# A two-layer graph kernel: layer 0 of all graphs first, then layer 1 in quads by two levels of Strassen

## The chip, the core and the metric

The kernel runs on one NeuronCore of a Trainium2 chip. The metric is the device time of one execution in microseconds (us). Everything is float32.

## The reference, cut to what matters

There are 128 graphs of 128 nodes with 512 features. `x` is [128, 128, 512], `adj` [128, 128, 128]. Both layers add their result to `x`.

```
# layer 0
h = relu(layernorm(x))
Xw = h @ Wv + bv;  sj = Xw @ aw[:512];  si = Xw @ aw[512:]
t = adj * exp(leaky_relu(sj[None, :] + si[:, None] + ab, 0.2));  t = t / (row sums of t + 1e-12)
H = (h @ Wk[0] + bk[0]) + (t @ h @ Wk[1] + bk[1]) + (t @ t @ h @ Wk[2] + bk[2])
x = x + relu(H)
# layer 1
h = relu(layernorm(x))
q, k = split(h @ Wqk);  v = h @ Wv1
w = rowsum(q * (adj @ (k * mask))) * mask / sqrt(512)
x = x + softmax(w over the nodes)[:, None] * v
```

The kernel never forms q and k. It folds the two halves of Wqk into one 512x512 matrix M, so that w is the row sum of (h @ M) * (adj @ h), scaled. Layer 1 is thus h @ [M, Wv1], a 512-deep product with 1024 columns, and one aggregation of h per graph.

## The kernel before, in words

Graphs are taken in pairs (G = 2, 64 pairs, p = 0 to 63). A dense product of a pair has two row blocks (the graphs), two halves of the 512-deep contraction and two halves of the columns. `strassen` (line 325) computes it with seven block products for eight, by the Winograd form. The left sums are made by `left_sums` (lines 313 to 323), four VectorE additions of 128x512 elements as two halves; the right sums are made once by `combine` (line 166). The seven products are accumulated in four PSUM banks a, b, c, e, and three copies by ScalarE (lines 343, 345, 347, 351) hand partial sums from one bank to the next. Each block product is two matrix instructions, one per 128-deep chunk (line 336). There are eight PSUM banks by name: set1 is a1, b1, c1, e1, and set2 is a2, b2, c2, e2.

For pair p, the work is this.

- `norm0(p)` (line 355): layer norm and relu (`norm_relu`, lines 255 to 281), written to DRAM and read back in 32x32 blocks (`by_blocks`, lines 288 to 297), so that `begin(p)` can transpose it on VectorE (line 302) and make the left sums.
- `y2(p)`: h @ Wk[2] with the attention columns, a Strassen product with 257-wide halves in set2. Then the column of sj is spread over the partitions: a small VectorE transpose into `pzt` (line 380), a DMA to DRAM `pzd` (line 382) and a DMA that reads it back on all partitions as `pz` (line 384), both issued by GpSimd.
- `attention(p)`: adds `pz` and si (line 398), leaky relu, exp, times adj, row sums, division; gives t. It also makes A^T of the pair by a VectorE transpose (line 412).
- `y10(p)`: h @ [Wk[1], Wk[0]], a Strassen product with 512-wide halves in set1, seeded with the biases (`seed_a`, `seed_e`); `t_transposed(p)` transposes t on TensorE within it.
- `inner(p)` and `outer(p)`: two times four products of 256 columns with t^T, then relu and the sum with x (line 73) into x1.
- `norm2`: layer norm of x1 into h2, and again the way through DRAM for its transpose.
- `layer1(p)`: h2 @ [M, Wv1], a Strassen product with 512-wide halves in set2, and two aggregations adj @ h2 of 512 columns, with A^T as the left side (line 474). `score` (line 560) takes the row sums, `spread_scores` (line 563) spreads them by way of DRAM, `weights` (line 575) makes the softmax, and `result` (line 593) multiplies, adds x1 and writes out.

The loop runs over p. Its body issues y10(p), inner(p), y2(p+1), the end of the layer 1 of pair p-2, outer(p), and then layer1(p-1) and attention(p+1). Layer 1 of the pair before thus stands between one pair's y2 and the next pair's y10. Tile pools hand out the buffers. The order of the instructions on each engine is set when the program is built: a scheduler with costs of its own orders them within the data dependencies, and `issue_after` pins some of them by hand (`behind`, line 70). At run time each engine takes its queue in that order.

## Time and profile before

| | |
|---|---|
| median of three runs | 2319.53 us (2315.21 to 2322.03) |
| profiled execution, its own time | 2314.45 us |
| span of the profiled execution, first to last instruction | 2312.7 us |
| TensorE (PE) busy | 2303.2 us |
| VectorE (DVE) busy | 1362.6 us |
| ScalarE (ACT) busy | 1026.8 us |
| GpSimd (POOL) busy | 341.9 us |
| data moved by DMA | 241.55 MB, 104 GB/s |

A group of the profile names line, engine, operation and tiles (output <- inputs), then the count, the busy time in us and the mean duration of one in ns, and last the time that the engine stood idle just before such instructions, with what released it. A matrix instruction in float32 leaves two records. PE durations overlap, since the matrix products are pipelined: the distance between starts is their pace.

### The profile page before, as it was taken

To read this page: it belongs to the slowest core of one execution; us is meant where nothing else is said; L and a number is where in the kernel's file an instruction comes from. 1 tells how busy PE (TensorE), PEld (TensorE's weight loads), DVE (VectorE), ACT (ScalarE), POOL (GpSimd) and SP (SyncE) were. 2 spreads that over 40 slices of the span, in tenths; PEclk is the share of its full clock that TensorE was granted. 3 is DMA by queue.
4 is the path that set the end of the run, shared out by engine and by line. 5 is a ranking of instruction groups with operands and counts; after the bars stand their busy time and mean duration, and the time that the engine had idled before them with its cause. 6 is when DMAs were issued, how large, how long until landed. Compare 5 with 4: busy or idle time off the path is not lost.

```text
span 2312.7 us, 23740 instructions
## 1 busy us (share of the span) xinstructions
PE 2303.2 (100%) x6889; PEld 1291.1 (56%) x6889; DVE 1362.6 (59%) x4134; ACT 1026.8 (44%) x2514; POOL 341.9 (15%) x595
## 2 busy tenths in 40 slices
PE   9999999999999999999999999999999999999999
PEld 5555555555555555555555555555555555555554
DVE  5665656655656566566565665565665656656654
ACT  4444444444444444444444444444444444444443
POOL 3011111111111111111111111111111111111100
PEclk9999999999999999999999999999999999999999
DMA  7343333333333333333333333333343333333321
GB/s 192 106 124 103 93 117 93 109 104 101 111 106 90 121 91 108 112 98 108 105 96 116 93 103 112 98 108 105 98 115 99 97 114 96 110 103 100 110 64 51
DMA packets 247060, 241.55 MB, mean 104 GB/s; under 512 B 25822, under 2 KB 171486, under 8 KB 246930
## 3 DMA queue, kind: packets, MB, share of 16 engines
q1 hardware_dynamic: 225632, 212.26, 30.4%
q0 software_dynamic: 21152, 27.65, 5.5%
q8 instruction: 54, 0.88, 0.2%
q14 instruction: 76, 0.62, 0.1%
q10 hardware_dynamic: 146, 0.14, 0.0%
HBM read 140.20 MB, written 99.74 MB: 104 GB/s over the span
## 4 chain that ended last, share of the span: by engine, by line
PE 98%; DMA 1%; DVE 1%; issue 0%; ACT 0%; POOL 0%; DVEq 0%; SPq 0%
PE b L336 24%; PE c L336 24%; PE a L336 24%; PE e L336 12%; PE a L474 2%; PE e L474 2%; PE a L452 1%; PE b L452 1%; PE b L462 1%; PE e L462 1%; PE c L452 1%; PE c L462 1%; PE e L452 1%; PE a L462 1%; PE a L423 1%; DMA t<-in_L_gnn_Wv_dram 1%
## 5 line engine op out<-in xcount | busy, mean ns | idle before, releaser
L336 PE MATMUL a<-r,x 128*128 128x257 f32 (+1 forms) x1024 | 372.7, 486 | 0.1
L93 POOL DMA_DIRECT2D agb<-in_adj_dram x256 | 152.2, 599 | 825.4 <-DVE t L409 780.3
L374 DVE TENSOR_TENSOR y<-e,s 128x257 f32<-128x257 f32 x64 | 27.3, 427 | 401.7 <-ACT s L351 401.7
L336 PEld LDWEIGHTS a<-r,x 128*128 128x128 f32 x1024 | 189.4, 190 | 105.8 <-issue 92.1
L336 PE MATMUL a<-rl,x 128*128 128x512 f32 x504 | 236.8, 592 | 0.0
L351 ACT COPY s<-c 128x512 f32<-128x512 f32 (+1 forms) x191 | 97.4, 510 | 207.9 <-PE c L336 207.8
L336 PE MATMUL b<-t,sx 128*128 128x257 f32 (+1 forms) x512 | 186.4, 486 | 2.7 <-ACT b L343 2.7
L336 PE MATMUL b<-r,sx 128*128 128x257 f32 (+1 forms) x512 | 186.5, 486 | 0.0
L336 PE MATMUL c<-t,sx 128*128 128x257 f32 (+1 forms) x512 | 186.4, 486 | 0.0
L336 PE MATMUL c<-t,x 128*128 128x257 f32 (+1 forms) x512 | 186.2, 486 | 0.0
L336 PE MATMUL e<-t,sx 128*128 128x257 f32 (+1 forms) x512 | 186.1, 486 | 0.0
L382 POOL DMA_DIRECT2D pzd<-pzt x62 | 36.9, 595 | 941.3 <-DVE pzt L380 910.6
L347 ACT COPY c<-b 128x512 f32<-128x512 f32 (+1 forms) x191 | 95.2, 499 | 179.1 <-PE b L336 177.6
L345 ACT COPY s<-e 128x512 f32<-128x512 f32 (+1 forms) x191 | 98.4, 515 | 156.2 <-PE e L336 156.2
L302 DVE STREAM_TRANSPOSE x<-hv 128x512 f32<-128x512 f32 x252 | 163.5, 686 | 1.9 <-DMA hv<-hd 1.7
L336 PEld LDWEIGHTS a<-rl,x 128*128 128x128 f32 x504 | 95.8, 190 | 93.2 <-issue 89.9
L268 DVE TENSOR_TENSOR r<-r 128x2 f32<-128x2 f32 x128 | 20.0, 156 | 203.2 <-ACT r L267 203.1
L343 ACT COPY b<-a 128x512 f32<-128x512 f32 (+1 forms) x191 | 95.6, 500 | 94.8 <-PE a L336 87.2
L336 PEld LDWEIGHTS b<-t,sx 128*128 128x128 f32 x512 | 97.1, 190 | 71.4 <-issue 46.4
L336 PEld LDWEIGHTS c<-t,x 128*128 128x128 f32 x512 | 97.0, 190 | 68.5 <-issue 61.2
L336 PEld LDWEIGHTS c<-t,sx 128*128 128x128 f32 x512 | 96.9, 190 | 68.6 <-issue 60.3
L336 PEld LDWEIGHTS e<-t,sx 128*128 128x128 f32 x512 | 96.9, 189 | 68.4 <-issue 60.7
(231 smaller groups left out, 3926.6 us busy)
## 6 DMA issues: line engine op xcount, KB each, us to landing
hd<-h SPq DMA_DIRECT2D x126, 512.0 KB, 2.8
hv<-hd SPq DMA_DIRECT2D x504, 128.0 KB, 2.9
xg<-in_x_dram SPq DMA_DIRECT2D x63, 512.0 KB, 3.8
out_dram<-x SPq DMA_DIRECT2D x63, 512.0 KB, 4.2
ag<-in_adj_dram SPq DMA_DIRECT2D x64, 128.0 KB, 2.6
agb<-in_adj_dram POOLq DMA_DIRECT2D x256, 32.0 KB, 2.1
pw<-pwd POOLq DMA_DIRECT2D x63, 128.0 KB, 3.3
pz<-pzd POOLq DMA_DIRECT2D x62, 128.0 KB, 3.5
```

The costliest lines, as they stand in the source:

```text
L93: nc.gpsimd.dma_start(agb[p][c * S32:(c + 1) * S32].rearrange("p g q i -> p (g q) i"), v[c])
L302: nc.vector.transpose(dst[:, j].rearrange("p f (n b) -> p f n b", n=Q), hv[:, j].rearrange("p n (f a) -> p f n a", f=Q))
L336: done["product"] = nc.tensor.matmul(bank, left[i][:, k * P:(k + 1) * P], right[i][:, k], start=(start and k == 0), stop=(k == HC - 1), sk ...
L343: nc.scalar.copy(b, a)
L345: nc.scalar.copy(s[:, 0], e)
L347: done["u2"] = nc.scalar.copy(c, b).ins
L351: nc.scalar.copy(s[:, 1], c)
L374: (1, 1): lambda e, t: nc.vector.tensor_add(y[:, 1, 1], e, t),
L382: nc.gpsimd.dma_start(d.rearrange("g q b -> q g b"), t[::S32])
L452: nc.tensor.matmul(bank[:, :HD], TT[p][:, j, :], y[:, j, nh, 1 - nh:W2 - nh], start=False, stop=True, skip_group_check=True)
L462: nc.tensor.matmul(bank[:, HD:], tt[:, j, :], z[:, j, nh], start=False, stop=True, skip_group_check=True)
L474: nc.tensor.matmul(to, AT[p][:, j, :], h2, start=True, stop=True)
```

## The change

Two loops take the place of one. The first runs layer 0 of all 64 pairs and ends each pair by writing four things to DRAM: h2 (`H2D`), its transpose (`XD`), the scaled A^T (`ATD`) and x1 (`X1D`). During pairs 2 to 9 the right side of layer 1 is worked out to the second level: seven matrices of 128x7x256 elements, kept in DRAM (`RWD`); four of them are loaded during pair 10, three after the loop.

The second loop takes four graphs (a quad, two pairs) at a time, 32 in all. The outer level of Strassen is over the two pairs and the halves of the contraction and gives seven factors; the inner level is over the two graphs of a pair and again halves. That is 49 products of a 128x128 left with a 128x256 right, one matrix instruction each. The outer factors 1, 5 are done in set1 and 2, 6 in set2 in step with each other, then the four aggregations, then 3, 7 in set1 and 4 in set2. The left sums are made in two levels, the outer ones on GpSimd (`load_left`), the inner on VectorE (`inner_sums`). Adding the outer factors up is left to VectorE and GpSimd (`adding_ends`). The scores of a quad are spread together, and the sum with x1 is made by an accumulating DMA from GpSimd's queue.

In the first loop, y2(p+2) follows outer(p), attention(p+1) follows y10(p), and the temporaries of y2 and y10 (`s2` and `s0` before) share one buffer `s`.

The core of the diff:

```diff
     def y2(p):
-        s = front.tile([P, 2, WP], FP, name="s2", bufs=1)[:, :, :W2]
+        s = front.tile([P, 2, WP * 2], FP, name="s", bufs=1)[:, :, :W2]
...
     def y10(p, steps):
-        s = front.tile([P, 2, D], FP, name="s0", bufs=1)
+        s = front.tile([P, 2, WP * 2], FP, name="s", bufs=1)[:, :, :D]
...
+    def for_layer1(p):
+        hT = front.tile([P, G, DC, N], FP, name="x2", bufs=1)
+        transposed(HV2.pop(p), hT)
+        for j in range(G):
+            nc.sync.dma_start(XD[p][:, :, j].rearrange("k p n -> p k n"),
+                              hT[:, j].rearrange("p (k f) n -> p k (f n)", k=2))
...
+    def norm2(p):
+        HV2[p] = by_blocks(norm_relu(X1[p]), H2D[p])
...
+    for p in range(NP):
+        def lefts():
+            if p == 0:
+                behind("t", begin, 1)
+                behind("left", norm0, 2)
+                return
             if p + 2 < NP:
+                begin(p + 2)
+            for_layer1(p - 1)
             if p + 3 < NP:
+                norm0(p + 3)
+
+        y10(p, {1: lefts, 6: lambda: behind("product", t_transposed, p)})
+        if 0 < p and p + 1 < NP:
+            attention(p + 1)
+        z = inner(p)
...
+        outer(p, z)
...
+        if p + 2 < NP:
+            y2(p + 2)
+        if p + 1 < NP:
+            seed_a()
+            seed_e()
+        norm2(p)
...
+    def load_left(q, pool):
+        f = F[q] = pool.tile([P, 8, G, HC, N], FP, name="f")
+        fv = f.rearrange("p o j k n -> p o (j k n)")
+        for o, p, kh in ((1, 2 * q, 0), (2, 2 * q, 1), (L21, 2 * q + 1, 0), (4, 2 * q + 1, 1)):
+            at = L21 if o == L21 else SLOT[o]
+            nc.sync.dma_start(fv[:, at], XD[p][kh].rearrange("p g n -> p (g n)"))
+        at = {o: fv[:, i] for o, i in SLOT.items()}
+        nc.gpsimd.tensor_add(at[5], fv[:, L21], at[4])
+        nc.gpsimd.tensor_sub(at[6], at[5], at[1])
+        nc.gpsimd.tensor_sub(at[3], at[2], at[6])
+        nc.gpsimd.tensor_sub(at[7], at[1], fv[:, L21])
+
+    def inner_sums(q, pool, first, n):
+        v = F[q][:, first:first + n]
+        s = pool.tile([P, 4, n, N], FP, name=f"in{first}")
+        b = {(j, k): v[:, :, j, k] for j in range(G) for k in range(2)}
+        nc.vector.tensor_add(s[:, 0], b[1, 0], b[1, 1])
+        nc.vector.tensor_sub(s[:, 1], s[:, 0], b[0, 0])
+        nc.vector.tensor_sub(s[:, 2], b[0, 0], b[1, 0])
+        nc.vector.tensor_sub(s[:, 3], b[0, 1], s[:, 1])
...
+    def adding_ends(to, other):
+        def one(i, j):
+            return lambda a: nc.vector.tensor_add(to(i, j), a, other(i, j))
+        def two(i, j):
+            def end(e, t):
+                nc.vector.tensor_add(t, e, t)
+                nc.gpsimd.tensor_add(to(i, j), t, other(i, j))
+            return end
+        return {(0, 0): one(0, 0), (1, 1): two(1, 1), (0, 1): two(0, 1), (1, 0): one(1, 0)}
...
+    def spread_scores(col):
+        t = small.tile([P, S32], FP, name="pwt", bufs=1)
+        nc.vector.transpose(t, col)
+        d = dram.tile([S32, Q, S32], FP, name="pwd")
+        nc.gpsimd.dma_start(d.rearrange("g q b -> q g b"), t)
+        dst = back.tile([P, 2 * G, N], FP, name="pw", bufs=1)
+        nc.gpsimd.dma_start(dst.rearrange("p g n -> p (g n)"), bcast(d, 0, 2 * G * N))
+        return dst
...
+    def result(q):
+        c, w = C.pop(q), W.pop(q)
+        factors = weights(w, spread_scores(w))
+        for pair in range(2):
+            v = c[:, pair].rearrange("p j h d -> p j (h d)")
+            for j in range(G):
+                at = pair * G + j
+                nc.scalar.activation(v[:, j], v[:, j], AF.Copy, scale=factors[:, at:at + 1])
+            p = 2 * q + pair
+            nc.gpsimd.dma_start(v, X1D[p].rearrange("g n d -> n g d"), accum_op=OP.add)
+            nc.sync.dma_start(out[p * G:(p + 1) * G].rearrange("b n d -> n b d"), v)
...
+    for q in range(NQ):
...
+        inner_sums(q, back, 4, 3)
+        together(one_round(q, set1, (1, 5), s1, plain_ends(lambda i, j: c[:, 0:2, i, j])),
+                 one_round(q, set2, (2, 6), s2, adding_ends(
+                     lambda i, j: c[:, 2:4, i, j],
+                     lambda i, j: c[:, 0:1, i, j].to_broadcast([P, 2, HD]))))
+        nc.vector.tensor_add(c[:, 0].rearrange("p j h d -> p (j h d)"), c[:, 3].rearrange("p j h d -> p (j h d)"),
+                             c[:, 1].rearrange("p j h d -> p (j h d)"))
+        for i, bank in enumerate((a1, a2, e1, e2)):
+            pair, j = divmod(i, 2)
+            ordered(lambda: nc.tensor.matmul(bank, AT[q][:, pair, j], H2[q][:, pair, j], start=True, stop=True))
+            nc.scalar.copy(agg[:, pair, j], bank)
+        scores(q, 0, c[:, 2])
+        if q > 0:
+            result(q - 1)
+        if q + 1 < NQ:
+            load_left(q + 1, fpools[(q + 1) % 2])
+            load_rest(q + 1)
+        together(one_round(q, set1, (3, 7), s1, adding_ends(lambda i, j: c[:, 0::3, i, j],
+                                                            lambda i, j: c[:, 0::3, i, j])),
+                 one_round(q, set2, (4,), s2, adding_ends(lambda i, j: c[:, 2:3, i, j],
+                                                          lambda i, j: c[:, 3:4, i, j])))
+        nc.gpsimd.tensor_add(c[:, 1].rearrange("p j h d -> p (j h d)"), c[:, 3].rearrange("p j h d -> p (j h d)"),
+                             c[:, 1].rearrange("p j h d -> p (j h d)"))
+        if q + 1 < NQ:
+            inner_sums(q + 1, early, 0, 4)
+        scores(q, 1, c[:, 2])
+    result(NQ - 1)
```

`one_round` issues seven products for its factors with the copies and ends of `strassen`; `together` puts the steps of two rounds side by side.

## The prediction

> **What bounds the kernel now.** I read the page's busy line and its chain first.
>
> ```profile
> PE 2303.2 (100%) x6889; PEld 1291.1 (56%) x6889; DVE 1362.6 (59%) x4134; ACT 1026.8 (44%) x2514; POOL 341.9 (15%) x595
> ...
> PE 98%; DMA 1%; DVE 1%; issue 0%; ACT 0%; POOL 0%; DVEq 0%; SPq 0%
> ```
>
> TensorE is never idle and is 98% of the chain. So the time is the number of matrix instructions times their pace, and the pace is in the timeline of PE alone, in the distances between starts.
>
> ```profile
> 1000.14 1.03 PE L336 MATMUL e<-t,sx 128*128 128x257 f32 x4
> 1001.01 1.03 PE L336 MATMUL b<-t,sx 128*128 128x257 f32 x4
> ...
> 1005.78 0.59 PE L462 MATMUL e<-zz,tt 128*128 128x256 f32 x2
> 1006.21 0.59 PE L462 MATMUL b<-zz,tt 128*128 128x256 f32 x2
> ...
> 1007.07 1.88 PE L336 MATMUL a<-rl,x 128*128 128x512 f32 x4
> 1008.79 1.88 PE L336 MATMUL e<-tl,sx 128*128 128x512 f32 x4
> ...
> 1042.56 1.88 PE L336 MATMUL a<-rl,x 128*128 128x512 f32 x4
> ```
>
> Four records are two instructions: 512 columns cost 1.717/2 = 0.858 us, 257 columns 0.433, 256 columns 0.432. A pair repeats every 35.49 us (1042.56 - 1007.07). Check: 28 x 0.858 + 14 x 0.433 + 8 x 0.432 + 2 x 0.858 (aggregations) + 0.22 (two transposes) = 35.5.
>
> Next, how full the others are while PE is full, from one 36 us window (PE, PEld, DVE, ACT, POOL, clock, DMA share, GB/s), and how long the spreading of the attention column takes, from the timeline of all engines.
>
> ```profile
> 1036.00:1072.00 36.00, 36.00 (x111) 20.34 (x110) 21.00 (x64) 16.07 (x40) 5.27 (x9) 1.00 0.37 108
> ```
>
> ```profile
> 1005.96 0.24 DVE L380 STREAM_TRANSPOSE pzt<-y 128x64 f32<-128x64 f32 x1 [0.20 <-ACT y L376]
> ...
> 1006.49 0.59 POOL L382 DMA_DIRECT2D pzd<-pzt  x1 [15.26 <-DVE pzt L380]
> ...
> 1008.42 0.57 POOL L384 DMA_DIRECT2D pz<-pzd  x1 [1.33 <-DMA pzd<-pzt]
> ...
> 1018.30 0.35 DVE L398 TENSOR_SCALAR s<-pz,y,cz 128x128 f32<-128x128 f32 x1
> ```
>
> ```profile
> pw<-pwd POOLq DMA_DIRECT2D x63, 128.0 KB, 3.3
> pz<-pzd POOLq DMA_DIRECT2D x62, 128.0 KB, 3.5
> ```
>
> pzt ends at 1006.20; pz is issued at 1008.42 and lands 3.5 us later, at 1011.9: a way of 5.7 us. VectorE takes pz up at 1018.30, so 6.4 us of slack lie behind it. Those 12 us are filled with twenty other VectorE instructions, many of them layer 1's.
>
> **What the Trainium skill says.** *GPSIMD Engine Reference*, 3.1: a two-input float32 `tensor_tensor` of 2048 elements takes 4497 ns on GpSimd, about 2.2 ns an element. The trace of before has no such instruction; I estimate 1.2 us for 512 elements and 2.3 for 1024. *SBUF — State Buffer*, Who interferes with whom: a VectorE instruction with two SBUF inputs contends with a GpSimd instruction that reads SBUF, and the second to start blocks until the first ends. No run here shows it; I leave it for the range. *TensorE: Matmul & The Clock Gate*, What's actually happening: an idle window of about 3.4 us can halve TensorE's clock. The trace only shows 1.00 with no gaps.
>
> **The change, part by part.**
>
> *Products.* A quad has 49 x 0.432 + 4 x 0.858 = 24.60 us, where two pairs had 56 x 0.432 in products and the same aggregations: 2.9 us less a quad. A pair of layer 0 keeps 14 x 0.858 + 6.06 + 3.46 + 0.22 = 21.75. Together 64 x 21.75 + 32 x 24.60 = 2179 for 64 x 35.49 = 2271: 92 us gained, if PE still sets the pace. The matrix rate for narrower products is not in doubt, since 256-wide ones already run at 0.432 back to back.
>
> *Layer 0 alone.* VectorE is 21.0 x 35.49/36 = 20.7 us busy per pair. Taking out layer 1's rows (left sums, two adds, scores, result, softmax; 7.1 by their means, 6.5 with the overlap of neighbours) and adding nothing, since h2's transpose stays, about 14.5 remain: 67% of 21.75. That fits by share, but not by order. I looked at how the built program orders VectorE's queue. Before, in 61 of 62 pairs 19 or 20 places lie from `pzt` to the first use of `pz`. Now it is the very next instruction in 22 pairs, 2 to 5 places on in 16, 6 to 10 in 20 (often the next pair's transposes and left sums, 2.6 us) and over 10 in 4. The queue is in order, so the 5.7 us are waited out: 22 x 5.7 + 16 x 4.5 + 20 x 3.1 = 259, or 4.2 us a pair. Behind this wait stand the next pair's transposes and left sums and the addition to e1 that `inner` needs, so TensorE gets it in full.
>
> Further waits of a middle pair, laid out by hand in queue order: `pzt` needs ScalarE's last copy of y2, which in half of the pairs stands behind the two h2 activations (2 x 0.76), 1.0 on average; VectorE waits for ln and exp of the norm, now behind a y2 copy, 1.7; the shared `s` puts y10's copies of e and c behind y2's end, and small dependent instructions 0.2 apart instead of 0.16, together 2.5. Sum: 14.5 + 4.2 + 1.0 + 1.7 + 2.5 = 23.9, taken as 24.0, a pair against 21.75 of PE. Lower bound 21.75, upper 27 (every pair with a full wait).
>
> DMA: about 4.2 MB a pair (x, adj twice, h and h2 out and back, h2^T, A^T, x1, pz) in 24 us is 173 GB/s, by 0.37 x 173/108 a share of 0.6. SP issues some 16 DMAs at 0.4 us (timeline), 7 of 24 us; h comes back within about 8 us and is used more than 10 later. Hidden, unless latencies grow; then pz's does too.
>
> *Second-level right sides.* 4 x 1.22 + 28 x 0.42 = 17 us of VectorE over eight pairs, which has no room left: 17.
>
> *Layer 1 alone.* Again there is a ring through VectorE's queue. `pwt`(q) is followed by two ends and then the maximum over pw(q). Between stand GpSimd's DMA to DRAM (0.2 + 0.6), then, ahead of the DMA that reads it back, the four outer left sums of a later quad (4 x 1.2 + 0.2), then that DMA (0.1 + 3.6 for twice the bytes of before): 9.6 us, of which none is needed sooner. From the maximum to the next `pwt` I lay out, in queue order: maximum 0.7, three ends 2.0, softmax with four exps 0.4, left sums and ends up to the second score 6.0; then VectorE waits for round 3, whose copies stand in ScalarE's queue behind four agg copies and four scalings of c (0.57 and 0.76 each, to 9.3), so that a1 ends at 12.2; seven ends to 17.2; the score waits for GpSimd's last additions, 19.1; two scores, one end, four sums and `pwt` to 23.2. Ring: 23.2 + 9.6 = 32.8, say 33 against 24.60. Without the additions between, and with ScalarE prompt, 25; with GpSimd and VectorE blocking each other, 36. 31 x 33 + 27 for the first = 1050. No row shows an accumulating DMA: between the 4.2 us of a plain write of 512 KB and twice that. It is issued some 10 us into the ring and its buffer c is wanted again 13 us or more later, write included, so I take nothing, and up to 2 us a quad for the upper end.
>
> *Ends.* Start as before, 33 us to the first y2. Between the loops 15: the last transposes and the three factors, 2.75 MB at the 231 GB/s of the first window (12). After the last product 18 more than before: score, two DMAs, softmax, four scalings, accumulating DMA, write.
>
> *Sum.* 33 + 64 x 24.0 + 17 + 15 + 1050 + 18 = 2669, as a span. Around the span lie 1.8 us (2314.45 - 2312.7), and the profiled run is 5 us under the median, so about 2675. I take 2670.
>
> **Rivals.** 0.3% is about what a measurement of this kernel can tell from no change.
>
> - *PE stays the bound* (faster). The mechanism is slack in buffers: x has three, h and y2 two, so VectorE may be carried ahead over the pz way, and in layer 1 the ends may lie under the next rounds. Then 2313 - 92 + 17 for the ends and 10 for the right sides = 2248. It decides if both rings come in under 21.75 and 24.60. For it: VectorE's share is 67% in layer 0 and about 80% in layer 1 (19.6 of 24.6 us, by the means of like rows). Against it: waits in an in-order queue are not share, and both rings close through VectorE. 4%.
> - *Only layer 0 loses*: the layer 1 ring under 24.6, 33 + 1536 + 17 + 15 + 787 + 18 = 2406. 11%.
> - *Only layer 1 loses*: 33 + 1392 + 17 + 15 + 1050 + 18 = 2525. 15%.
> - *Both, and worse*: pz late under 0.6 DMA share, the engines' lock, TensorE's clock halved after gaps over 3.4 us: 27 and 36 give 33 + 1728 + 17 + 15 + 1143 + 18 = 2954. 9%.
> - *Both as worked out*: 2670, from 2560 to 2800. 61%.
>
> That the change doesn't do what it says is excluded: the built queue has 49 products a quad.
>
> **How the numbers follow.** The likeliest is 2670. Leaving out the first case, most of the second and the upper half of the fourth gives 2450 to 2880. Faster 0.04, within 0.3% 0.01, slower 0.95.
>
> **What would show it.** Layer 0: the use of pz with a wait for DMA in VectorE's list, 3 to 6 us for many pairs; PE idle before `inner` with VectorE as releaser; pair distance near 24. Layer 1: the maximum waiting for pw; quad distance near 33; PE's product distance 0.432 throughout. Wrong: PE near 100% in either loop, GpSimd additions far from 1.2 us, or a wait for hv or f, which would be DMA.

## The result, and the profile after

The changed kernel takes 2886.99 us (median of four runs, 2883.29 to 2889.57), where the kernel before took 2317.66 us beside it (median of four). The ratio is 1.245, with a 95% interval of 1.243 to 1.248. That is slower, as forecast, by 7 us more than the upper end of the range (2880) and by 217 us more than the value (2670).

From the page of the changed kernel, the busy line, TensorE's clock in 40 slices, and the chain:

```profile
PE 2438.2 (84%) x8223; PEld 1585.9 (55%) x8223; DVE 1588.1 (55%) x4223; ACT 1236.3 (43%) x2929; POOL 791.3 (27%) x886
...
PEclk9999999999999999999999998989898989888887
...
issue 12%; POOL 11%; PE 10%; DMA 7%; DVE 7%; ACT 5%; POOLq 0%; SPq 0%; ACTq 0%; DVEq 0%
```

TensorE was 98% of the chain and is now 10% of it; the other shares of the line go round between all engines and the DMA. No engine is full. So the time lies in engines that wait for one another. Where such waits close into a ring (each waits for the next and the last for the first), the length of the ring is the pace, and the question is where it closes. The first product of layer 1 starts at 1730.09 us, so the two loops can be read apart. From the view by stretches (PE, PEld, DVE, ACT, POOL, then clock, DMA share, GB/s):

```profile
36.00:1730.00 1694.00, 1497.79 (x4740) 893.27 (x4739) 924.08 (x3009) 738.85 (x1782) 220.95 (x376) 0.96 0.57 163
1730.00:2888.00 1158.00, 909.39 (x3394) 674.20 (x3392) 647.13 (x1163) 485.42 (x1124) 555.88 (x476) 0.88 0.50 135
```

A pair of layer 0 takes (1730 - 33)/64 = 26.5 us (26.3 without the 17 us forecast for the right sides), forecast 24.0. Layer 1 takes 1158 us, forecast 15 + 1050 + 18 = 1083. VectorE is busy 55 and 56%.

*Layer 0.* The list of waits between 100 and 1750 us (engine, line and tile, releaser: total, times, longest):

```profile
DVE z L418 <- DMA pz<-pzd: 417.4, 60, 10.5
...
PE c L349 <- ACT s L364: 103.3, 47, 5.7
```

VectorE waits 7 us for `pz` in nearly every pair. How TensorE gets it is seen in the timeline of one pair, around 1300 us:

```profile
1295.92 0.25 DVE L401 STREAM_TRANSPOSE pzt<-y 128x64 f32<-128x64 f32 x1 [1.51 <-ACT y L397]
...
1301.72 0.60 POOL L405 DMA_DIRECT2D pz<-pzd  x1 [4.69 <-DMA pzd<-pzt]
1305.53 0.60 DVE L418 TENSOR_SCALAR z<-pz,y,cz 128x128 f32<-128x128 f32 x2 [9.36 <-DMA pz<-pzd]
1307.57 3.53 PE L349 MATMUL c<-t,x 128*128 128x512 f32 x4 [2.40 <-ACT s L364]
```

`pzt` is ready at 1296.2, and VectorE does nothing until 1305.5. The exp of the attention stands ahead of a copy in ScalarE's queue and waits for `z`, so the copy comes late and TensorE stands idle 2.40 us; then it runs at half pace (3.53 us for four records that took 1.88 in the profile shown before). The way from the end of `pzt` to the landing of `pz` took 5.7 us in the pair that the prediction read, and 6.0 in the mean over 62 pairs of the kernel before. Here it is 8.7 in the mean. The list of DMAs shows it too (count, KB, median us from issue to landing), first from the changed kernel's page, then from the kernel before between 700 and 1500 us:

```profile
pz<-pzd POOLq DMA_DIRECT2D x62, 128.0 KB, 4.3
pzd<-pzt POOLq DMA_DIRECT2D x62, 1.0 KB, 3.3
...
pzd<-pzt POOLq DMA_DIRECT2D x22, 1.0 KB, 1.7
```

`pz` lands in 4.3 us, where it was 3.5; the write of 1 KB ahead of it takes 3.3, where it was 1.7.

*Layer 1.* The list of waits between 1800 and 2880 us:

```profile
DVE peak L731 <- DMA pw<-pwd: 262.6, 31, 9.3
...
PE e L797 <- DVE s L715: 146.6, 30, 5.6
```

and one turn of the ring in the timeline:

```profile
2203.05 0.20 DVE L746 STREAM_TRANSPOSE pwt<-wcol 128x32 f32<-128x32 f32 x1
...
2203.56 0.76 POOL L748 DMA_DIRECT2D pwd<-pwt  x1 [3.86 <-DVE pwt L746]
2204.34 1.27 POOL L613 TENSOR_TENSOR f<-f 128x512 f32<-128x512 f32 x1
...
2209.45 0.60 POOL L750 DMA_DIRECT2D pw<-pwd  x1
2213.02 0.69 DVE L731 TENSOR_REDUCE peak<-pw 128x4 f32<-128x512 f32 x1 [8.60 <-DMA pw<-pwd]
...
2214.36 2.08 PE L797 MATMUL e<-h,at 128*128 128x512 f32 x2 [4.95 <-DVE s L715]
...
2232.02 2.35 POOL L811 TENSOR_TENSOR c<-c 128x1024 f32<-128x1024 f32 x1
2232.10 2.83 DVE L760 SCALAR_TENSOR_TENSOR junk<-agg,wscale,c 128x512 f32<-128x512 f32 x1 [2.38 <-POOL c L716]
```

Between the two DMAs stand four GpSimd additions (the first is shown). The maximum waits 8.60 us, the end of e2 stands behind it, and TensorE's fourth aggregation, which needs that bank, waits for that end 4.95 us. After the gap TensorE runs at half pace (2.08 us for two records of 512 columns, else 1.02). A quad takes 34.7 us (mean of 31 distances between maxima), forecast 33.

So both mechanisms of the prediction are there, and both cost more than it gave them. What remained to be shown is that they are the cause of the time, and what is late next without them.

### The profile page after: what moved, and what is told of

Read it like the earlier page. It is cut to its first block, busy times and chain, and to the rows that moved or that the text cites. A ratio compares the mean times of both kernels' runs of the same rounds, so it can differ in the third digit from the quotient of the medians.

```text
span 2887.8 us, 29075 instructions
## 1 busy us (share of the span) xinstructions
PE 2438.2 (84%) x8223; PEld 1585.9 (55%) x8223; DVE 1588.1 (55%) x4223; ACT 1236.3 (43%) x2929; POOL 791.3 (27%) x886
## 4 chain that ended last, share of the span: by engine, by line
issue 12%; POOL 11%; PE 10%; DMA 7%; DVE 7%; ACT 5%; POOLq 0%; SPq 0%; ACTq 0%; DVEq 0%
DMA pw<-pwd 4%; POOL c L716 3%; POOL c L811 2%; PE a L667 2%; DVE s L715 2%; ACT c L772 2%; PE b L667 2%; PE e L667 1%; DMA pzd<-pzt 1%; POOL f L613 1%; POOL f L611 1%; DMA pz<-pzd 1%; POOL f L610 1%; ACT agg L798 1%; PE c L667 1%
## 5 line engine op out<-in xcount | busy, mean ns | idle before, releaser
L349 PE MATMUL a<-r,x 128*128 128x512 f32 (+1 forms) x1024 | 387.3, 499 | 16.1 <-ACT a L450 14.7
L716 POOL TENSOR_TENSOR c<-s,c 128x512 f32<-128x512 f32 x192 | 205.5, 1083 | 335.7 <-DVE s L715 281.1
L667 PE MATMUL a<-rw,f 128*128 128x256 f32 x896 | 259.2, 429 | 33.5 <-ACT agg L798 30.3
L418 DVE TENSOR_SCALAR z<-pz,y,cz 128x128 f32<-128x128 f32 x124 | 38.7, 343 | 419.0 <-DMA pz<-pzd 419.0
L667 PEld LDWEIGHTS a<-rw,f 128*128 128x128 f32 x896 | 183.7, 212 | 124.4 <-POOL c L716 51.3
L667 PE MATMUL b<-rw,in 128*128 128x256 f32 x896 | 219.1, 385 | 10.3 <-ACT b L672 10.3
L797 PE MATMUL e<-h,at 128*128 128x512 f32 x128 | 96.9, 850 | 151.5 <-DVE s L715 151.5
L760 DVE SCALAR_TENSOR_TENSOR junk<-agg,wscale,c 128x512 f32<-128x512 f32 x128 | 161.5, 1262 | 83.5 <-POOL c L716 75.7
L667 PEld LDWEIGHTS b<-rw,in 128*128 128x128 f32 x896 | 172.6, 194 | 41.1 <-ACT b L672 16.7
L734 ACT ACTIVATE ej<-pw,peak 128x128 f32<-128x128 f32 x128 | 49.8, 390 | 314.2 <-DVE peak L731 314.2
```

Of the source, the lines that this page charges most:

```text
L349: done["product"] = nc.tensor.matmul(bank, left[i][:, k * P:(k + 1) * P], right[i][:, k], start=(start and k == 0), stop=(k == HC - 1), sk ...
L418: nc.vector.tensor_scalar(z[:, j, :], pz[:, j, :], y[:, j, 1, HD:], cz, op0=OP.add, op1=OP.add)
L667: ordered(lambda: nc.tensor.matmul(bank[:, at * HD:(at + 1) * HD], left1(q, o, i), RW[o][:, RIGHT[i]], start=start and at == 0, stop=True, ...
L716: nc.gpsimd.tensor_add(to(i, j), t, other(i, j))
L734: nc.scalar.activation(ej, pw[:, j, :], AF.Exp, bias=peak[:, j:j + 1], accum_out=w[:, 2, j:j + 1])
L760: nc.vector.scalar_tensor_tensor(junk, agg[:, pair, j], wscale[:, b:b + 1], y[:, j].rearrange("p h d -> p (h d)"), op0=OP.mult, op1=OP.mul ...
```

## The experiments

All numbers are read as above: the end of layer 0 is the start of the first product of layer 1, a pair is the median distance between `pzt`, a quad the median distance between maxima. Line numbers are shifted a little against the changed kernel. Totals of a single run are given without an interval. Four of these kernels have the same order of VectorE's queue in layer 0 (the changed one, `pw` read ahead, maximum later, short addition), and their layer 0 ends between 1718 and 1730: differences of that size in one run say nothing. Where an expectation below names another length of a quad than this table (33.2, 28.5, 26.4), it is the mean of the same run, not the median.

| kernel | layer 0 ends | pair | quad | total us |
|---|---|---|---|---|
| changed kernel | 1730 | 26.3 | 34.8 | 2887 |
| pz used later | 1524 | 22.0 | 35.0 | 2690 |
| pw read ahead of the sums | 1718 | 26.5 | 33.5 | 2832 |
| maximum later | 1726 | 26.4 | 33.1 | 2830 |
| writes left out | 1574 | 23.3 | 34.8 | 2731 |
| writes of 4 partitions | 1671 | 25.7 | 34.7 | 2828 |
| short addition | 1720 | 26.4 | 34.1 | 2843 |
| both loops reordered | 1472 | 22.0 | 33.7 | 2586 |
| ... addition on VectorE | 1469 | 22.0 | 33.7 | 2581 |
| copies first | 1472 | 22.0 | 31.1 | 2517 |
| ... addition on VectorE | 1477 | 22.0 | 28.2 | 2442 |
| two temporaries | 1474 | 22.0 | 26.9 | 2376 |
| softmax later | 1471 | 22.0 | 24.7 | 2317 |
| short tail | 1475 | 22.0 | 24.9 | 2313 |

### pz used later

```diff
-            (0, 1): lambda b, t: ... nc.vector.tensor_add(b, b, t),
+            (0, 1): lambda b, t: done.update(y10=(... nc.vector.tensor_add(b, b, t)).ins),
...
-            nc.vector.tensor_scalar(z[:, j, :], pz[:, j, :], y[:, j, 1, HD:], cz, op0=OP.add, op1=OP.add)
+            if p > 1:
+                behind("y10", nc.vector.tensor_scalar, z[:, j, :], pz[:, j, :], y[:, j, 1, HD:], cz, OP.add, OP.add)
```

> From the changed kernel, only the place of attention's first use of pz in VectorE's queue is moved: it is pinned behind the addition of y10's first column half to b1, so that in most pairs 12 to 13 instructions stand between pzt and it. My theory (the 6.8 us a pair waited for pz are the wait of an in-order queue, and TensorE gets them in full): the wait for pz falls below 1 us a pair, the pair comes down from 26.5 to 22 to 23 us, and the total from 2887 to 2600 to 2680. Rival (VectorE's own work, the busy DMA or the clock limits layer 0, and the wait for pz only hides it): the wait comes back under another name, and the total stays at 2830 or above. Layer 1 is the same under both: 1158 us.

2690.35 us. From 700 to 1500 us of this kernel, by stretches and in the timeline of one pair:

```profile
700.00:1500.00 800.00, 798.20 (x2688) 498.69 (x2689) 507.53 (x1690) 418.15 (x1010) 121.25 (x209) 1.00 0.67 191
```

```profile
1152.22 0.70 DVE L466 TENSOR_TENSOR e<-e,s 128x512 f32<-128x512 f32 x1 [3.49 <-ACT s L364]
1154.77 0.57 DVE L83 TENSOR_SCALAR z<-pz,y,cz 128x128 f32<-128x128 f32 x2
```

TensorE is busy 798 of 800 us at full clock, and this `z` no longer waits, 11 us after `pzt` (1143.9); over all pairs its waits for `pz` are 50 us, 0.8 a pair. The addition to e1 that `inner` needs now stands ahead of `z`. One pin takes 206 us out of layer 0. The wait for `pz` was thus most of the loss of layer 0, and VectorE's 63% share was enough for TensorE's 22.0 us. The total is 10 us above the range of the expectation, because pairs 9 to 30, whose queue is less regular, still took 21 to 32 us: there `z` remained three to five places behind `pzt` in many pairs.

### Less DMA beside it

```diff
-        for j in range(G):
+        for j in range(G if p < 2 else 0):
             nc.sync.dma_start(XD[p][:, :, j]...
...
-        nc.sync.dma_start(ATD[p], aT)
+        if p < 2:
+            nc.sync.dma_start(ATD[p], aT)
...
-            nc.sync.dma_start(AT[q][:, i], ATD[p])
+            nc.sync.dma_start(AT[q][:, i], ATD[p % 2])
```

> From the changed kernel, the writes of h2 transposed, A^T and x1 to DRAM are left out for pairs 2 to 63, and layer 1 reads those of pairs 0 and 1 again; the output is not the reference's, all instructions on the four compute engines are the same, and layer 0 moves about 28% fewer bytes. Theory (the way of pz takes 8.9 us where the kernel before had 5.7 because of the DMA load of layer 0): the way falls to 7 to 8 us, the pair by 1 to 2 us, the total to 2760 to 2830. Rival (the longer way comes from GpSimd's queue or is set by the round trip itself): way and pair as in the changed kernel, the total within 20 us of 2887.

2730.56 us, 30 us below the expected range. It isn't a clean test: the builder's scheduler ordered VectorE's queue anew, with `z` ten places behind `pzt`. So the same was tried with the DMAs in place but small, which leaves the order as it was (A^T and x1 are cut in the same way):

```diff
+        few = P if p < 2 else 4
         for j in range(G):
-            nc.sync.dma_start(XD[p][:, :, j].rearrange("k p n -> p k n"),
-                              hT[:, j].rearrange("p (k f) n -> p k (f n)", k=2))
+            nc.sync.dma_start(XD[p][:, :few, j].rearrange("k p n -> p k n"),
+                              hT[:few, j].rearrange("p (k f) n -> p k (f n)", k=2))
...
```

> From the changed kernel, the writes of h2 transposed, A^T and x1 to DRAM carry only 4 of 128 partitions for pairs 2 to 63, and layer 1 reads those of pairs 0 and 1 again, so that the output is not the reference's. All instructions and their order on every engine are those of the changed kernel (in the run that left the writes out the order of VectorE's queue had changed with it: pz was used 10 places behind pzt, not 1 to 6). Theory (DMA load stretches the way of pz): pz lands in 3.5 us for 4.3, the way falls from 8.8 to 7.3 to 7.8, and the pair by as much, 1.0 to 1.5 us: layer 0 ends 65 to 95 us earlier, total 2790 to 2825. Rival (the order was what helped in that run): layer 0 ends within 25 us of 1730, total above 2860.

2828.2 us, and layer 0 ends 59 us earlier: near the theory but short of its range (65 to 95 us), and beyond the rival's. The landing times with the writes left out:

```profile
pz<-pzd POOLq DMA_DIRECT2D x62, 128.0 KB, 3.5
pzd<-pzt POOLq DMA_DIRECT2D x62, 1.0 KB, 2.8
```

With small writes they are 3.8 and 3.0. In the mean the way is 8.7 us in the changed kernel (163 GB/s in layer 0), 8.1 with small writes (127 GB/s), 7.5 with the writes left out (133 GB/s and fewer DMAs). So the writes do stretch the way: that of `pz` itself wholly (3.5 us without them, as in the kernel before, though in the run whose order had changed), that of the 1 KB write in part (2.8; it was 1.7).

The rate isn't the measure, though: the reordered kernels below move 196 GB/s in layer 0, with a way of 8.6 to 8.8 us. What goes with the landing times is the number of other DMAs in flight, that is, those between issue and landing at the same time. Beside the 1 KB write there are 1.3 of them in the mean in the kernel before and 7.2 in the changed kernel. Within the changed kernel the six such writes with at most three others beside them landed in 1.8 us in the mean, the other 56 in 3.7. With the writes left out 5.2 remain, 3.2 of them reads of h2, and the 1 KB write takes 3.0 in the mean. That goes with the 1 us which the writes don't explain; no run tests it by itself. The Trainium skill (*DMA: Bandwidth & Descriptors*, Latency and other measured facts) says that HBM access takes 0.2 us on average and 2 us at high load, and that this dominates the fixed cost of a small DMA; the direction agrees, 1.7 to 3.3 us for 1 KB, but no run here separates the memory from the DMAs ahead in the queues.

### pw read ahead of the sums

```diff
+        def sums():
             nc.gpsimd.tensor_add(at[5], fv[:, L21], at[4])
...
+        if "pw" in done:
+            behind("pw", sums)
...
-        nc.gpsimd.dma_start(dst.rearrange("p g n -> p (g n)"), bcast(d, 0, 2 * G * N))
+        done["pw"] = nc.gpsimd.dma_start(dst.rearrange("p g n -> p (g n)"), bcast(d, 0, 2 * G * N)).ins
```

> From the changed kernel, only the four outer left sums on GpSimd are moved: they now stand behind the DMA that reads pw, not ahead of it. My theory (pwt to maximum is 9.85 us because four additions of 1.27 us stand between the two DMAs in GpSimd's queue): pwt to maximum falls to 6.2 to 6.6, the ring from 34.7 to 30.5 to 31.5, the total to 2765 to 2800. Rival (GpSimd's later additions of c, now 5 us later, or VectorE's left sums wait instead): the ring stays above 33.5 and the total above 2850. Layer 0 is the same under both.

2831.83 us, a quad of 33.5: between the two. From `pwt` to the maximum it takes 6.6 us, as expected, but 1.9 of the 3.2 us gained came back. In the timeline:

```profile
2282.09 1.14 DVE L741 TENSOR_TENSOR wcol<-wcol,peak 128x4 f32<-128x4 f32 x1
...
2283.26 0.20 ACT L742 ACTIVATE wcol<-wcol 128x4 f32<-128x4 f32 x1 [0.73 <-DVE wcol L741]
...
2284.08 2.04 PE L672 MATMUL a<-rw,f 128*128 128x256 f32 x4 [1.93 <-ACT agg L803]
```

ScalarE's four exps, which wait for the maximum, and one more exp stand ahead of the copy of an aggregation that TensorE needs. That last exp waits for a VectorE addition of four columns, which takes 1.14 us beside GpSimd's additions to c (0.27 in the changed kernel).

### The maximum later

```diff
-        nc.vector.tensor_reduce(peak, pw, AX.X, OP.max, negate=True)
+        behind("score", nc.vector.tensor_reduce, peak, pw, AX.X, OP.max, True)
...
-        c = C[q] = back.tile([P, 4, G, 2, HD], FP, name="c", bufs=2)
+        c = C[q] = back.tile([P, 4, G, 2, HD], FP, name="c", bufs=3)
```

> From the changed kernel, the maximum over pw is moved from the third place behind pwt in VectorE's queue to behind the last score of the next quad (14 places); c has three buffers instead of two, since the result is now formed later. My theory (the 9.85 us of the spreading are waited for by VectorE, and through it by TensorE, only because of the maximum's place): the wait for pw vanishes, the quad takes 27.5 to 29.5 us, the total is 2660 to 2720. Rival (ScalarE's queue, with four scalings of c in the midst of the next round's copies, or GpSimd's chain, is nearly as long): 32 to 34 us a quad, 2800 to 2860.

2830.24 us, a quad of 33.1: the rival's number. The wait for `pw` is gone, and another has its place:

```profile
2291.48 0.40 ACT L734 ACTIVATE ej<-pw,peak 128x128 f32<-128x128 f32 x1 [3.23 <-DVE peak L83]
...
2296.98 2.93 PE L667 MATMUL c<-rw,in 128*128 128x256 f32 x6 [5.30 <-ACT c L680]
```

ScalarE's exps wait for the maximum in the midst of round 3, four scalings follow, and the copy of b to c that TensorE needs stands behind both.

### The lock of VectorE and GpSimd

```diff
-        nc.gpsimd.tensor_add(c[:, 1]..., c[:, 3]..., c[:, 1]...)
+        nc.gpsimd.tensor_add(c[:, 1]...[:, :16], c[:, 3]...[:, :16], c[:, 1]...[:, :16])
```

> From the changed kernel, GpSimd's addition of 128x1024 elements to c at the end of a quad is cut to 16 elements a partition, so that the output is not the reference's; all else, and the order on every engine, is the same. Theory (GpSimd's addition blocks the score on VectorE, which takes 2.83 us beside it and 0.74 alone, and the score is in the ring): the score falls to 0.74 and the ring from 34.7 by 1.5 to 2.5 us to 32.2 to 33.2, total 2810 to 2840. Rival (the 2.83 us are a wait for the addition's data or are not in the ring): ring and total unchanged within 0.5 us and 20 us.

2842.84 us, 3 us outside the theory's range, and a quad of 34.1, between theory and rival. In the timeline:

```profile
2478.46 0.75 DVE L760 SCALAR_TENSOR_TENSOR junk<-agg,wscale,c 128x512 f32<-128x512 f32 x1 [2.37 <-POOL c L716]
```

The score takes 0.75 us for 2.83: the blocking that the prediction left for the range is real. But the ring falls by 0.7 us in the median (1.1 in the mean), not by 2.1. This lock's share of the ring is thus about 1 us; where the other half went isn't settled by this run.

### Both loops reordered

The first use of `pz` is also pinned behind the left sums of a later pair. In layer 1 (core of the diff):

```diff
+                with tc.issue_after(done["left"]):
+                    behind("y10", nc.vector.tensor_scalar, z[:, j, :], pz[:, j, :], ...)
...
+        if "gadd" in done:
+            behind("gadd", sums)
...
+            at = ("cp1", "cp5", "cp6", "cp6")[j] if "cp1" in done else "mm"
+            with tc.issue_after(done[at]):
+                nc.scalar.activation(ej, pw[:, j, :], AF.Exp, ...)
...
+                with tc.issue_after(done["cp7"]):
+                    nc.scalar.activation(v[:, j], v[:, j], AF.Copy, scale=factors[:, at:at + 1])
```

Here cp1 to cp7 are ScalarE's copies of a round, gadd is GpSimd's last addition of a round.

> From the changed kernel, only the order is changed, in both loops. Layer 0: the first use of pz is pinned behind y10's addition to b1 and behind the left sums of a later pair (12 or more places behind pzt in nearly all pairs). Layer 1: the maximum stands behind the scores of the next quad's first half (15 places), the exps stand one by one behind ScalarE's copies of round 3, the scalings behind its last copy, GpSimd's left sums behind its additions of the first two rounds, VectorE's inner sums behind the first scores, the accumulating DMAs behind GpSimd's additions; c has three buffers. My theory (both loops lose only to waits of in-order queues, which the order can take away): layer 0 at 22 to 22.5 us a pair ends near 1450 to 1490 (it ended at 1730, and at 1524 with the first pin alone), a quad takes 25 to 28 us, the total is 2300 to 2430. Rival (in layer 1 VectorE and GpSimd are full once their mutual blocking is counted, so that order can't help much): 30 us a quad or more, total above 2480.

2585.53 us, ratio 1.116 (1.114 to 1.117). Layer 0 ends at 1472, as expected. Layer 1 doesn't follow: 33.7 us a quad, the rival's number. The rival's reason (VectorE and GpSimd full, counting their blocking) is only half of what the timeline shows:

```profile
2036.26 4.73 DVE L806 TENSOR_TENSOR c<-c 128x1024 f32<-128x1024 f32 x1 [3.01 <-POOL c L725]
...
2040.91 1.75 DVE L771 SCALAR_TENSOR_TENSOR junk<-agg,wscale,c 128x512 f32<-128x512 f32 x1
...
2045.96 0.40 ACT L745 ACTIVATE ej<-pw,peak 128x128 f32<-128x128 f32 x1 [7.03 <-DVE peak L83]
...
2047.38 2.93 PE L676 MATMUL c<-rw,in 128*128 128x256 f32 x6 [6.32 <-ACT c L689]
...
2066.80 0.58 POOL L761 DMA_DIRECT2D pw<-pwd  x1 [4.53 <-DMA pwd<-pwt]
...
2069.87 1.26 POOL L615 TENSOR_TENSOR f<-f 128x512 f32<-128x512 f32 x1
2069.94 4.73 DVE L806 TENSOR_TENSOR c<-c 128x1024 f32<-128x1024 f32 x1 [2.62 <-POOL c L725]
```

The exps wait 7 us ahead of the copy that TensorE needs, and GpSimd holds its additions 4.5 us behind a DMA that nobody needs yet: that is order. But the maximum for which the exps wait stands on VectorE behind an addition and a score that GpSimd stretches to 4.73 and 1.75 us (1.22 and 0.74 alone): that is the blocking. The run beside it moves the last addition to VectorE:

> As the run beside it (both loops reordered), but the addition of 128x1024 elements to c at the end of a quad is done by VectorE instead of GpSimd. If the blocking of VectorE by GpSimd costs more than the addition itself (1.2 us on VectorE), a quad is 0.5 to 2 us shorter and the total 15 to 60 us below the run beside it; if VectorE is simply full, 0.5 to 1.2 us a quad longer, 15 to 40 us above; if TensorE is the bound in both, within 10 us.

2581.31 us, ratio 1.113 (1.110 to 1.116), 4 us less: with TensorE waiting for ScalarE's copy, it doesn't matter.

### Copies first

```diff
-            at = ("cp1", "cp5", "cp6", "cp6")[j] if "cp1" in done else "mm"
+            at = "cp7" if "cp1" in done else "mm"
...
+                with tc.issue_after(done["mm" if last else ("cp1", "cp5", "cp6", "cp7")[at]]):
+                    nc.scalar.activation(v[:, j], v[:, j], AF.Copy, scale=factors[:, at:at + 1])
...
+        with tc.issue_after(done["gadd"]):
+            done["pw"] = nc.gpsimd.dma_start(dst.rearrange("p g n -> p (g n)"), bcast(d, 0, 2 * G * N)).ins
```

The scalings are now issued a quad later. The maximum also moves, behind VectorE's inner sums, and GpSimd's left sums stand behind the DMA that reads `pw`.

> From the run with both loops reordered (2585 us, 33.2 us a quad), three things move in layer 1: the exps stand behind ScalarE's last copy of round 3 (they stood ahead of two copies of it and held them 7 us, waiting for the maximum), the scalings one by one behind copies of the next quad's first rounds, and GpSimd issues the DMA that reads pw behind its additions of the first two rounds (it had held them 4.5 us) and the accumulating DMAs behind its left sums. My theory (a ring of in-order waits): a quad takes 25.5 to 28.5 us, the total is 2340 to 2440. Rival (VectorE and GpSimd are full, counting how they block one another; taking ScalarE's wait away only uncovers that): above 30 us a quad, above 2490.

2516.66 us, ratio 1.087 (1.085 to 1.088), 31.1 us a quad: 2.6 less, but again the rival's number. With the addition on VectorE:

> As the run beside it, with the addition of 128x1024 elements at the quad's end on VectorE instead of GpSimd. If VectorE and GpSimd set the pace: 0.5 to 2 us a quad less, 15 to 60 us below the run beside it; if VectorE alone sets it, as much longer; if TensorE or ScalarE does, within 10 us.

2442.02 us, ratio 1.054 (1.051 to 1.056), 28.2 us a quad. Now the same edit that did nothing gives 75 us, more than expected, and 2.9 us a quad for an instruction of 2.35 us on GpSimd and 1.22 on VectorE. By the expectation's own reading VectorE and GpSimd set the pace here, as the rival had it, with the addition at the quad's end in the middle of it. Neither was full by its share: VectorE was busy 503 and GpSimd 359 of 650 us (from 1600 to 2250 us, ahead of this edit).

### Two temporaries

In this kernel TensorE waited once a quad, 2.8 us, for a copy behind a scaling that waited for VectorE.

```diff
-        s1 = back.tile([P, 2, D], FP, name="s1", bufs=1)
+        s1 = back.tile([P, 2, D], FP, name="s1", bufs=2)
...
-                with tc.issue_after(done["mm" if last else ("cp1", "cp5", "cp6", "cp7")[at]]):
+                with tc.issue_after(done["mm" if last else ("e00", "cp7", "cp7", "e10")[at]]):
```

e00 and e10 are the two ends that ScalarE copies in rounds 1 and 2.

> From the reordered kernel with the addition on VectorE (2442 us, 28.5 us a quad, TensorE waiting only once a quad, 2.8 us, for ScalarE's copy of b to c), three things move: the temporaries s1 and s2 have two buffers each (ScalarE's copy of e had waited for GpSimd to read the old one), the four scalings of c stand behind later copies of the next quad (one had waited 2.6 us for VectorE ahead of that copy), and h2 and A^T of the first quad are read ahead of the last three right sides. My theory (the waits of in-order queues are the whole of layer 1's loss): a quad takes 24.7 to 26, TensorE is busy throughout, the total is 2330 to 2370. Rival (VectorE, 19 to 20 us of work a quad and some 5 to 8 of being blocked by GpSimd, is the next bound): 27.5 us a quad or more, total 2405 to 2440.

2375.94 us, ratio 1.025 (1.022 to 1.027), 26.9 us a quad, between the two and nearer to the theory. Which of the three moves gave how much isn't separated. The next wait:

```profile
1936.82 0.69 DVE L631 TENSOR_TENSOR in<-f 128x512 f32<-128x512 f32 x1 [1.15 <-POOL f L616]
...
1942.62 1.99 PE L679 MATMUL a<-rw,f 128*128 128x256 f32 x8 [1.45 <-DVE c L723]
```

VectorE's inner sums wait for GpSimd's left sums, and the end of a that frees TensorE's bank stands behind them.

### The softmax later

```diff
-            behind("score", inner_sums, q + 1, early, 0, 4)
+            behind("ae", inner_sums, q + 1, early, 0, 4)
...
+        behind("dadd", nc.vector.tensor_reduce, PEAK[q], PW[q], AX.X, OP.max, True)
...
+            with tc.issue_after(done["mm" if last else ("cp1", "cp5", "cp6", "e00")[j]]):
+                nc.scalar.activation(ej, pw[:, j, :], AF.Exp, ...)
```

ae and dadd are VectorE's last ends of a and of b in round 3; the exps belong to the next quad's rounds.

> From the run at 2376 us (26.4 us a quad), the order of layer 1 is moved once more: VectorE's inner sums and the maximum, which stood ahead of round 3's ends and waited for GpSimd's left sums, now stand behind the ends of a and of b; GpSimd's left sums stand ahead of the DMA that reads pw; the exps and the scalings stand one by one behind copies of the next quad's first two rounds. My theory: the last wait of TensorE in a quad (1.5 us, for VectorE's end of a) goes, a quad takes 24.6 to 25.2 us, TensorE's own pace, and the total is 2315 to 2345, level with the kernel before or up to 1% above it, because what is then left is the join of the two loops and some slower pairs early in layer 0. Rival (VectorE with its blocking is as long as TensorE): 26 us a quad or more, 2365 or above.

2316.97 us, ratio 1.0003 (0.999 to 1.001): level with the kernel before, as expected. The page's busy line, and a stretch of layer 1:

```profile
PE 2242.4 (97%) x8223; PEld 1539.4 (66%) x8223; DVE 1605.5 (69%) x4255; ACT 1240.9 (54%) x2929; POOL 804.9 (35%) x854
```

```profile
1560.00:2250.00 690.00, 688.11 (x2942) 553.56 (x2941) 592.82 (x1030) 425.73 (x974) 499.55 (x388) 1.00 0.70 192
```

TensorE is busy 688 of 690 us at full clock, a quad takes 24.7, and VectorE is busy 86%. The products, the DMA traffic and the arithmetic are those of the changed kernel; only the order, the number of some buffers and the engine of one addition differ. So the 570 us were order, buffers and the place of that addition (75 us), and not the amount of work.

### The tail

```diff
-            nc.scalar.activation(v[:, j], v[:, j], AF.Copy, scale=factors[:, at:at + 1])
-        nc.gpsimd.dma_start(v, X1D[p].rearrange("g n d -> n g d"), accum_op=OP.add)
-        nc.sync.dma_start(out[p * G:(p + 1) * G].rearrange("b n d -> n b d"), v)
+            nc.vector.scalar_tensor_tensor(v[:, j], v[:, j], factors[:, at:at + 1], x1l[:, pair, j], op0=OP.mult, op1=OP.add)
+            nc.sync.dma_start(out[p * G + j], v[:, j])
```

for the last quad alone, with x1 read into a free buffer.

> From the run at 2317 us, only the end of the last quad is changed: x1 of its four graphs is read into SBUF ahead, VectorE does scaling and sum in one instruction a graph (four of about 0.75 us), and each graph is written out by itself, in place of four scalings on ScalarE, two accumulating DMAs (6 us to landing) and two writes of 512 KB. If the tail (34 us from the last product to the end) is this chain, it falls by 7 to 10 us and the total to 2306 to 2311, just below the kernel before (2316). Rival (the tail is set by the spreading of the scores and the last additions, and the accumulating DMA was overlapped): less than 3 us, total 2313 to 2318.

2312.61 us, ratio 0.998 (0.996 to 0.999): just below the kernel before. From the last product to the end of the span it is 26 us (2284.9 to 2310.8), 34 in the run above (2283.2 to 2317.0): the tail was this chain, and falls by 8 us as expected. The total falls by 4 only, between theory and rival; in the profiled executions layer 0 ended 4 us later than in the run above.

## Why the prediction was right and wrong

*What bounds the kernel, and the products.* Right. A pair takes 22.0 us and a quad 24.7 where TensorE is the bound, for 21.75 and 24.60. By these figures 73 of the 92 us are there (64 x 35.49 - 64 x 22.0 - 32 x 24.7); the order of the changed kernel does not let them be had.

*Layer 0: the step that failed is "a way of 5.7 us".* Measured are 26.5 us over 64 pairs, forecast 23.9. VectorE works 14.4 of it (forecast 14.5), waits 6.5 for `pz` (forecast 4.2) and 5.5 for all else (forecast 5.2). That last sum came out nearer than its parts: 0.8 us for y (forecast 1.0), 1.2 for the norm (1.7), 3.5 for the rest (2.5); TensorE's half pace, for which nothing was taken, is somewhere in it. With a way of 8.7, the table of queue places in the prediction gives 22 x 8.7 + 16 x 7.5 + 20 x 6.1 = 433 us, where 419 were waited. So the places were read rightly, and the duration was wrong. It came from a kernel with a DMA share of 0.37 and was used in one with 0.57. The prediction named this ("unless latencies grow; then pz's does too") and put it in a rival of 9%, while its own estimate of the share, 0.6, said that the load would be there. The wait is 419 - 259 = 160 us longer than forecast, more than the whole excess of layer 0, 1730 - (33 + 1536 + 17) = 144. That this wait set the pace is shown by the pin, which brings most pairs down to TensorE's own 22.0 us; why the way grew is shown in part (the writes) and in part argued (the DMAs in flight).

*Layer 1: the mechanism was right, the ring a little short.* From `pwt` to the maximum 9.8 us (forecast 9.6, though the terms given for it add up to 9.5); the additions on GpSimd took 1.26 to 1.28 us (estimate 1.2). From the maximum to the next `pwt` 24.9 (forecast 23.2). Left out of the value were the lock, about 1 us by the run with the short addition, and TensorE's half pace after each gap. "PE's product distance 0.432 throughout" was wrong: just after a gap two records of 512 columns took 2.08 us, else 1.02, and the clock was at half for 232 of the 1081 us between 1775 and 2856. How much of that lies in the ring wasn't measured. A quad of 34.7 for 33 makes 1.7 x 31 = 53 of the 75 us by which layer 1 was late.

*The ends.* The join was near: first quad 44.8 us (1730.1 to 1774.9) for 15 + 27. After the last product it takes 31 us (2856.6 to 2887.8), where the kernel before took 4 (2308.5 to 2312.7): 27 more, forecast 18.

*Accumulating DMA at nothing.* Right for the ring of the changed kernel, in which no compute engine waits for a buffer of `c` to come free. (In the last two kernels, with three buffers, ScalarE waits 9 and 14 us in all for the write of `c`.) In the tail it cost: 6.3 us to landing, and then a write.

*The rivals.* "Both, and worse" gave 27 and 36, and 2954. The truth lies between it and the value, and nearer to the rival: 67 us for 217. "PE stays the bound" at 2248 had 4%, and the runs rule it out for this order only. The reordered kernel with the short tail has a span of 2311 us. Of the 63 us above 2248, 40 lie in layer 0 (1475 for 33 + 1392 + 10), whose first half is less regular, and 23 in the join, layer 1 and the tail.

*Where a stall goes, and what is late next.* The prediction asked this once, for the change. The experiments had to ask it five times in layer 1: `pw`, then ScalarE's exps, then GpSimd's additions behind a DMA, then a scaling, then GpSimd's sums. Several expectations of mine failed for lack of it: `pw` read ahead of the sums (31.5 us at most expected, 33.5 measured), the later maximum (29.5 at most, 33.1), the first reordering (28 at most, 33.7), the second (28.5 at most, 31.1) and the two temporaries (26 at most, 26.9). Each time part or all of the gain was taken by something that I had not laid out: the next queue, and in the two reorderings also the blocking between VectorE and GpSimd.

## What to carry to other kernels

A duration of a DMA round trip belongs to the load it was measured under; where a change puts more DMAs in flight beside it (here 7.2 for 1.3), take a longer one as the value, not as the tail of the range. When a step with a long DMA way is moved, count the places between the start of the way and its first use in each in-order queue, and pin the use behind work that is due anyway: one pin was worth 206 us here. A wait in a ring is only gone when the queue of every engine in it has been laid out; take away one and the next takes its place, here often at nearly the same length. And where two engines block one another, an instruction can cost more than its own time: moved from GpSimd to VectorE, an addition of 1.22 us gave 2.9 us a quad.

## What the runs showed of the hardware

- A VectorE addition of 128x1024 elements, 1.22 us alone, took 4.73 us beside GpSimd's additions in the first reordering: it started at 2069.94, 0.07 us after the first of four, and was passed by three of them (1.26 us each). The Trainium skill (*SBUF — State Buffer*, Who interferes with whom) says that the ports which the two share are an exclusive lock: who issues first has them for the whole instruction, and the other blocks. The score beside one long addition agrees (2.83 us for 0.75), but here the wait went on over several instructions. GpSimd's sums in turn took 1.7 to 1.8 us for 1.26 beside VectorE in the run with two temporaries.
- TensorE ran at half pace after an idle time of 2.40 us (3.53 us for 1.88). The Trainium skill (*TensorE: Matmul & The Clock Gate*, What's actually happening) names a window of about 3.4 us; a shorter gap was enough here, though not always. Of the changed kernel's idle times that began at full clock, none of the 45 between 0.7 and 1.5 us was followed by half pace within 0.8 us, 6 of the 17 between 2 and 3 us were, and all 41 above 4 us.
- An accumulating DMA of 512 KB from DRAM into SBUF took 6.2 to 6.8 us to landing in most kernels and 8.1 and 9.2 in the first reordering and the run beside it (medians); a plain read of 512 KB (h2) took 4.3 to 4.7, a plain write (of the output) 3.7 to 3.9.
